# A graph layer on one core: transfers of the lengths moved to ScalarE, ten tiles fetched by rows, two hot quads summed last

## The chip, the core and the metric

The kernel runs on one core of a Trainium2 chip. A core has TensorE (PE, with its weight loads PEld), VectorE (DVE), ScalarE (ACT), GpSimd (POOL) and SyncE (SP). The metric is the device time of one execution in microseconds, less being better. Three runs of the kernel before took 719.8, 721.39 and 721.6 us, with a median of 721.39.

## The reference, cut to what matters

```python
width = CUTOFF / NUM_RBF * 0.5                    # 10 / 50 * 0.5
centers = jnp.linspace(0.0, CUTOFF, NUM_RBF)
rbf = jnp.exp(-(distances[:, None] - centers) ** 2 / (2.0 * width * width))
cut = 0.5 * (jnp.cos(jnp.pi * distances / CUTOFF) + 1.0) * (distances <= CUTOFF)
W = (silu(rbf @ fw1 + fb1) @ fw2 + fb2) * cut[:, None]
messages = (h[src] @ pw + pb) * W
agg = segment_sum(messages, dst, num_segments=num_atoms)
x = h + (silu(agg @ mw1 + mb1) @ mw2 + mb2)
out = (x - mean(x)) / sqrt(var(x) + 1e-05)        # over the last axis
```

There are 400,000 edges, sorted by `dst`, and 12,500 nodes of 128 numbers. An edge has a source, a destination and a length. Edges longer than 10 have `cut` 0 and add nothing. The weights are 128x128 (`fw1` is 50x128).

## The kernel before, in words

**Lists.** The edges come in seven chunks. For each chunk DVE finds the edges that are near enough and where each belongs in a shorter list; POOL scatters sources, destinations and lengths to a table `packed` in DRAM (L507); SP reads the shortened list back as `pair` (two transfers, L834); DVE unpacks it (`unpack`, which begins with `two`, L852, then L853), and SP stores the lengths as `near_d` in DRAM (L911). The table is cleared beforehand by transfers of zeros (`clear_packed`, L229). From here on edges stand in 139 quads, each four tiles of 128 edges. A chunk becomes 11 to 27 quads, and chunk 3 begins at quad 46, chunk 4 at 69, chunk 5 at 91, chunk 6 at 114.

**The loop over quads.** For a quad, POOL gathers the 128 projected source rows of each tile by an indirect transfer (`fetch`, L1074; the tables `proj`, or `in_x_dram` in the beginning). For the quads in `SINGLY` tile 0 is left out there; SP fetches its 128 rows instead, one transfer of 512 bytes each (`one_by_one`, L1064), and before each 32 of them loads 32 addresses into registers (L1060, TENSOR_LOAD). For each pair of quads (number `o`), SP fetches the lengths, spread over partitions (`radial`, L1093, the tile `d`, three buffers); ACT makes the radial basis (L1121, L1122); PE multiplies (L1130); ACT takes silu (L1136); PE makes the filter (L1144, L1147). DVE multiplies filter and gathered rows (`message`, L1158) and makes the one-hot matrix (`place`, L1170); PE sums (`sum_up`, L1190), and DVE adds the sum to the node's column (`add`, L1223). When a stretch of nodes has all its sums, the node stages follow (L1233 to L1292).

**What sets the order.** The order of instructions on each engine is written out (`manual_schedule`); an engine runs its list from first to last. A small planner in the code decides between which steps the rows of `one_by_one` stand: a clock in the planner adds `A_ROW` for each row. DVE's `two` of chunk 3 stands right after the message of quad 26, a full 20 quads before it is wanted. POOL's gathers each wait for a sum some steps back, and for the buffer they write.

**Completion semaphores.** Each transfer that SP or ACT issues signals one of eight semaphores, `DMAHW0` to `DMAHW7`. They are given out in turn, in the order in which the whole program is written, over both engines together; and a transfer is not issued before the last one that had the same semaphore has landed. So transfer number m waits for number m-8. In the rows below this wait stands in brackets.

Of the kernel before, what the change touches and what calls it, by code (L numbers as in the profile page):

```python
# [10 lines left out]
F32 = mybir.dt.float32  # L11
# [33 lines left out]
LAST = 26  # L45
# [11 lines left out]
OTHERS = 4, 5, 6, 7  # L57
OWN_4 = 66
# [13 lines left out]
SINGLY = (22, 44, 62, 67, 86, 102, 118, 133)  # L72
A_ROW = .58
# [6 lines left out]
READY = {80: 9, 84: 6, 88: 5, 90: 4}  # L80
# [6 lines left out]
def kernel(  # L87
# [61 lines left out]
    def load_x(t0, n=None):  # L149
        t = x4_sb[loaded[0] % X_BUFS]  # L150
        loaded[0] += 1
        node_dma(t0, t, x, False, n)
        x_sb[t0] = t
# [26 lines left out]
    def quad_of(q):  # L180

        return q if q < LAST or q >= NL else LAST if q == NL - 1 else q + 1

    def steps(k):

        return k if k <= LAST or k >= NL else k - 1

# [35 lines left out]
    def clear_packed(k, eng):  # L223
        a, b = CLEAR[k:k + 2]
        for i in range(LISTS if k == 0 else 3):
            v = packed[i, a:b].rearrange("(p w) -> p w", p=P)
            for w0 in range(0, (b - a) // P, 376):
                n = min(376, (b - a) // P - w0)
                eng.dma_start(v[:, w0:w0 + n], zero_i[:, :n])  # L229
# [594 lines left out]
    def unpack(c):  # L824
# [109 lines left out]
        if mine:  # L934
            at_row = work.tile([64, P], I32, name="at_row", bufs=2)
            nc.vector.tensor_scalar(at_row[:np_], f_src[:, :P], float(4 * H), None, op0=OP.mult)
            for q in mine:
                p = 2 * (quad_of(q) - QB[c])
                singles.extend((q, e, at_row[p:p + 1]) for e in range(P))
# [17 lines left out]
        if QB[c] <= LAST < QB[c + 1]:  # L957
            k = 2 * (LAST - QB[c])
            upto, that = (work.tile([64, 1], F32, name=n, bufs=1)[:np_] for n in ("upto", "that"))
            nc.vector.scalar_tensor_tensor(that, ident[:np_, k:k + 1], -1.0, ident[:np_, k + 1:k + 2],  # L960
                                           op0=OP.mult, op1=OP.subtract)
# [87 lines left out]
    singles, alone, rows_at, row_at = [], {}, [], [0.0]  # L1049
# [38 lines left out]
    def radial(o, lengths, eng=nc.sync):  # L1088

        n = math.prod(lengths.shape) // QE  # L1090
        d = work.tile([P, QE], F32, name="d", bufs=3)
        v = lengths.rearrange("(o h) e -> o h e", o=1)
        eng.dma_start(d, v.to_broadcast([64, 2, QE]))  # L1093
        d_of[o] = d, n
# [3 lines left out]
    def radials(to):  # L1098

        while next_o[0] < min(to, -(-NL // 2)):  # L1100
# [3 lines left out]
            a, b = 2 * quad_of(quads(o)[0]), 2 * quad_of(quads(o)[-1]) + 2  # L1104
            assert b - a == 2 * len(quads(o))
            radial(o, near_d[a:b].rearrange("(h t) e -> h (t e)", t=2))
# [99 lines left out]
    def bases_of(q0, q1):  # L1206

        _, v = nc.values_load_multi_w_load_instructions(
            base_i[0:1, 2 * quad_of(q0):2 * quad_of(q1 - 1) + 2], engines=[mybir.EngineType.DVE],
            min_val=0, max_val=N - min(wide(q) for q in range(q0, q1)),  # L1210
            skip_runtime_bounds_check_because="bases are destinations, and end in the table")
        for k in range(2 * (q1 - q0)):
            bases[q0 + k // 2, k % 2] = v[k]

    def added(q):

        return max((q - 2) // 2 * 2 if q < NL - 14 else q - 1 if q < NL - 4 else q, 0)
# [85 lines left out]
    def finish(every):  # L1303

        for t0 in every:
            load_x(t0)
# [5 lines left out]
            normalize(*ready.pop(0), on=range(QT))  # L1312
# [33 lines left out]
    def nodes(q):  # L1346
# [21 lines left out]
        if q == NL - 7:  # L1368
            st_of[3] = statistics()
            node_stats(80, st_of[3])  # L1370
        if q == NL - 4:
            node_stats(84, st_of[3][:, 4:])
        if q == NL - 3:
            node_stats(88, st_of[3][:, 8:])
# [3 lines left out]
    def last_step(q, msg):  # L1378

        assert not ready and not deep and not singles  # L1380
        bases_of(q, NL - 1)
        roots = deviations([84, 88, 90], st_of[3][:, 4:])
# [3 lines left out]
        keep_busy(5)  # L1386
        sum_up(q, msg)
        assert done_to(2 * q + 2) >= 95 * P
        node_first(93)
# [7 lines left out]
        node_first(95)  # L1397
        last(1)
        normalize(*ready.pop(0))
# [339 lines left out]
```

## Time and profile before

| | |
|---|---|
| runs | 719.8, 721.39, 721.6 us |
| the profiled execution | 719.15 us, span 717.5 us |
| granted TensorE clock | 0.917 |
| PE, PEld | 590.3 us (82%), 465.0 us (65%) |
| DVE | 561.8 us (78%) |
| ACT | 397.3 us (55%) |
| POOL | 536.4 us (75%) |
| gathers of POOL (L1074) | 548 |
| rows fetched by SP (L1064) | 1024 |
| transfers of `d` (L1093) | 70, all on SP |

The span is counted from the first to the last instruction; the time of the execution is 1.65 us longer. Busy time of an engine leaves out the issuing of transfers on SP and ACT, register work and waits. "SPq" and "ACTq" are the queues on which these engines issue transfers. A wait is put down to the work that ended last before it.

### The profile page before, as it was taken

To read this page: it belongs to the slowest core of one execution; us is meant where nothing else is said; L and a number is where in the kernel's file an instruction comes from. 1 tells how busy PE (TensorE), PEld (TensorE's weight loads), DVE (VectorE), ACT (ScalarE), POOL (GpSimd) and SP (SyncE) were. 2 spreads that over 40 slices of the span, in tenths; PEclk is the share of its full clock that TensorE was granted. 3 is DMA by queue.
4 is the path that set the end of the run, shared out by engine and by line. 5 is a ranking of instruction groups with operands and counts; after the bars stand their busy time and mean duration, and the time that the engine had idled before them with its cause. 6 is when DMAs were issued, how large, how long until landed. Compare 5 with 4: busy or idle time off the path is not lost. (4 is left out here: it accounts for less than half of the span.)

```text
span 717.5 us, 13667 instructions
## 1 busy us (share of the span) xinstructions
PE 590.3 (82%) x3524; PEld 465.0 (65%) x3524; DVE 561.8 (78%) x1736; ACT 397.3 (55%) x564; POOL 536.4 (75%) x576
## 2 busy tenths in 40 slices
PE   6887877898889889888588896999987878878884
PEld 5775556776667667576466674787765655656663
DVE  8899799787988999899689895878655455565685
ACT  6557624563645566464348253858744833574474
POOL 7777777777777777777777777777777777777773
PEclk9999687997988999999979997999998999999998
DMA  8995442343334334343333343444433433244342
GB/s 263 348 324 174 149 128 75 87 137 100 98 86 121 97 95 108 97 128 83 94 106 113 98 119 103 137 127 135 136 97 99 148 92 114 84 141 134 96 130 91
DMA packets 53389, 91.35 MB, mean 127 GB/s; under 512 B 13856, under 2 KB 21120, under 8 KB 53306
## 3 DMA queue, kind: packets, MB, share of 16 engines
q1 hardware_dynamic: 34754, 53.20, 22.9%
q0 software_dynamic: 17840, 36.77, 19.8%
q8 instruction: 29, 0.48, 0.3%
q10 hardware_dynamic: 712, 0.46, 0.2%
q14 instruction: 54, 0.44, 0.2%
HBM read 74.59 MB, written 15.79 MB: 126 GB/s over the span
## 5 line engine op out<-in xcount | busy, mean ns | idle before, releaser
L1074 POOL DMA_INDIRECT quad<-proj,srci x421 | 400.6, 952 | 128.4 <-issue 97.6
L1147 PEld LDWEIGHTS bank<-fw_sb,s 128*128 128x128 f32 x1112 | 160.8, 208 | 66.5 <-issue 59.8
L1136 ACT ACTIVATE s<-ph 128x1024 f32<-128x1024 f32 x70 | 71.3, 1018 | 184.4 <-PE ph L1130 184.3
L1147 PE MATMUL bank<-fw_sb,s 128*128 128x128 f32 x1112 | 161.8, 293 | 0.0
L1130 PE MATMUL ph<-rbf,w_sb 102*128 102x512 f32 x278 | 147.1, 655 | 7.5 <-ACT rbf L1122 3.9
L1190 PEld LDWEIGHTS sums<-hot,msg 128*128 128x128 f32 x816 | 112.0, 204 | 54.9 <-issue 27.4
L1170 DVE TENSOR_SCALAR hot<-iota_n,dl,cut 128x80 f32<-128x80 f32 (+4 forms) x408 | 110.1, 344 | 23.6 <-PE sums L1190 21.7
L1190 PE MATMUL sums<-hot,msg 128*128 128x80 f32 (+4 forms) x816 | 113.7, 285 | 15.4 <-DVE msg L1156 7.7
L1144 PE MATMUL bank<-fb_b,ones_b 96*128 96x512 bf16 x139 | 56.1, 404 | 48.8 <-DVE msg L1158 29.8
L1074 POOL DMA_INDIRECT x<-proj,srci x79 | 75.0, 949 | 24.1 <-issue 19.8
L1158 DVE TENSOR_TENSOR msg<-bank,quad 128x512 f32<-128x512 f32 (+1 forms) x82 | 55.7, 679 | 39.4 <-DMA quad<-proj,srci 36.9
L1130 PEld LDWEIGHTS ph<-rbf,w_sb 102*128 102x128 f32 x278 | 52.8, 211 | 48.1 <-issue 38.8
L1223 DVE TENSOR_TENSOR aggT<-aggT,sums 128x80 f32 (+4 forms) x209 | 54.0, 258 | 32.5 <-PE bank L1234 11.7
L1121 ACT ACTIVATE rbf<-d,rbf_bias,rbf_scale 102x512 f32<-102x512 f32 x70 | 56.2, 803 | 14.8 <-DMA d<-near_d 14.7
L1074 POOL DMA_INDIRECT quad<-in_x_dram,srci x48 | 47.6, 992 | 14.8 <-issue 11.9
L347 PEld LDWEIGHTS bank<-pw_sb,xT 128*128 128x128 f32 (+1 forms) x292 | 42.0, 207 | 8.0 <-issue 4.0
L1122 ACT ACT_TABLE_LOAD x35 | 44.9, 1283 | 0.6
L1136 ACT ACT_TABLE_LOAD x35 | 44.9, 1283 | 0.6
L1122 ACT ACTIVATE rbf<-rbf 102x512 f32<-102x512 f32 x70 | 44.1, 630 | 1.5
L1190 PE MATMUL sums<-quad,quad 128*128 128x104 f32 (+3 forms) x296 | 40.9, 281 | 3.9 <-DVE quad L1158 3.9
L1170 DVE TENSOR_SCALAR quad<-iota_n,dl,cut 128x104 f32<-128x104 f32 (+3 forms) x148 | 40.5, 348 | 3.9 <-issue 2.8
L1158 DVE TENSOR_TENSOR quad<-bank,quad 128x512 f32<-128x512 f32 (+2 forms) x40 | 25.2, 632 | 23.4 <-DMA quad<-proj,srci 16.1
(282 smaller groups left out, 803.0 us busy)
## 6 DMA issues: line engine op xcount, KB each, us to landing
d<-near_d SPq DMA_DIRECT2D x70, 256.0 KB
dl<-proj SPq DMA_DIRECT2D x1024, 0.5 KB
x<-in_x_dram SPq DMA_DIRECT2D x45, 256.0 KB
quad<-proj,srci POOLq DMA_INDIRECT x421
proj<-hp SPq DMA_DIRECT2D x24, 256.0 KB
out_dram<-x SPq DMA_DIRECT2D x21, 256.0 KB
r_d<-in_edge_weight_dram SPq DMA_DIRECT2D x5, 256.0 KB
r_dst<-in_dst_dram SPq DMA_DIRECT2D x5, 256.0 KB
```

What stands on the lines that cost most here:

```text
L347: nc.tensor.matmul(to[:m, k, :], lT[:, k * P:k * P + m], w, start=False, stop=(k == a + c - 1))
L1074: ins = nc.gpsimd.indirect_dma_start(out=got[:, j, :], out_offset=None, in_=proj if table is None else table, in_offset=bass.IndirectOffse ...
L1121: nc.scalar.activation(rbf[:u], d[:u], AF.Square, bias=rbf_bias[:u], scale=rbf_scale[:u])
L1122: nc.scalar.activation(rbf[:u], rbf[:u], AF.Exp, scale=-1.0 / (2.0 * width * width))
L1130: nc.tensor.matmul(ph[:, h, :], w1_sb[:2 * KR, h, :], rbf[:2 * KR], start=True, stop=True)
L1136: nc.scalar.activation(s[:, :n], ph[:, :n], AF.Silu)
L1144: nc.tensor.matmul(pu, ones_b[:, :P], bias_b["fb2"].rearrange("k j f -> k (j f)"), start=True, stop=False)
L1147: nc.tensor.matmul(pu[:, j * H:(j + 1) * H], s[:, j * P:(j + 1) * P], fw2_sb, start=False, stop=(j == QT - 1))
L1158: nc.vector.tensor_mul(msg[:, a:b, :], pu_of[q].rearrange("p (j f) -> p j f", j=QT)[:, a:b, :], got_of[q][:, a:b, :])
L1170: nc.vector.tensor_scalar(hot[:, j, :wide(q)], iota_n[:, :wide(q)], dl[:, at[0], at[1]], cut[:, at[0], at[1]], op0=OP.is_equal, op1=OP.mult)
L1190: ins = nc.tensor.matmul(pa[:, k * W:k * W + wide(q)], msg[:, j, :], hot[:, j, :wide(q)], start=(j % n == 0), stop=(j % n == n - 1))
L1223: nc.vector.tensor_add(to, to, pa[:, k * W:k * W + wide(q)])
```

## The change

The text has five parts.

1. `SINGLY` grows from eight quads to ten, at other places; `A_ROW` goes from .58 to .48. SP then fetches the rows of ten tiles, 1280 in all, instead of 1024, and POOL makes two gathers fewer, 546 instead of 548.
2. `radial` issues the transfer of `d` from ACT for o >= 8, and one step earlier (`q // 2 + 6`).
3. `clear_packed` clears the same columns of all its lists with one transfer from zeros that are read over and over: 14 transfers become 4.
4. Two quads (25 and 26) are summed last instead of one (26). Both add to one window of the node columns, in node tile 3 (`END`).
5. The tail after the last quad is rewritten: the node tiles 93 and 95 are done before the last sum, the last tile's bias and doubled input are put into PSUM beforehand, and its normalization uses one statistic, one root, one reciprocal and one TENSOR_SCALAR.

The diff, cut:

```diff
-LAST = 26
+LAST = 25
+N_LAST = 2
+OWN_D = 8
-SINGLY = (22, 44, 62, 67, 86, 102, 118, 133)
-A_ROW = .58
+SINGLY = (22, 34, 43, 60, 74, 86, 99, 113, 126, 137)
+A_ROW = .48
-READY = {80: 9, 84: 6, 88: 5, 90: 4}
+READY = {80: 9, 84: 7, 88: 6, 90: 5, 93: 4, 95: 3}
...
     def clear_packed(k, eng):
         a, b = CLEAR[k:k + 2]
-        for i in range(LISTS if k == 0 else 3):
-            v = packed[i, a:b].rearrange("(p w) -> p w", p=P)
-            for w0 in range(0, (b - a) // P, 376):
-                n = min(376, (b - a) // P - w0)
-                eng.dma_start(v[:, w0:w0 + n], zero_i[:, :n])
+        m = LISTS if k == 0 else 3
+        v = packed[:m, a:b].rearrange("s (p w) -> p s w", p=P)
+        for w0 in range(0, (b - a) // P, 376):
+            n = min(376, (b - a) // P - w0)
+            eng.dma_start(v[:, :, w0:w0 + n], zero_i[:, None, :n].to_broadcast([P, m, n]))
...
     def radial(o, lengths, eng=nc.sync):
-        n = math.prod(lengths.shape) // QE
         d = work.tile([P, QE], F32, name="d", bufs=3)
-        v = lengths.rearrange("(o h) e -> o h e", o=1)
-        eng.dma_start(d, v.to_broadcast([64, 2, QE]))
-        d_of[o] = d, n
+        for h, v in enumerate(lengths):
+            v = v.rearrange("(o h) e -> o h e", o=1)
+            if len(lengths) == 1:
+                eng.dma_start(d, v.to_broadcast([64, 2, QE]))
+            else:
+                eng.dma_start(d[h::2], v[:, 0, :].to_broadcast([64, QE]))
+        d_of[o] = d, sum(math.prod(v.shape) for v in lengths) // QE
...
-            radial(o, near_d[a:b].rearrange("(h t) e -> h (t e)", t=2))
+            at = [quad_of(q) for q in quads(o)]
+            by = at[-1] - at[0] if len(at) > 1 else 1
+            v = near_d.rearrange("(h t) e -> h (t e)", t=2)
+            radial(o, [v[at[0]:at[-1] + 1:by]] if by > 0 else [v[a:a + 1] for a in at],
+                   nc.scalar if o >= OWN_D else nc.sync)
...
-        radials(q // 2 + 5)
+        radials(q // 2 + 6)
...
-    def last_step(q, msg):
+    def last_step(q):
-        bases_of(q, NL - 1)
-        roots = deviations([84, 88, 90], st_of[3][:, 4:])
+        node_second(95)
+        node_stats(95, st_of[1][:, 11:])
+        msg = message(q)
+        nc.scalar.activation(warm, half_pi, AF.Sqrt)
+        roots = deviations([84, 88, 90, 93, 95], st_of[1])
...
-        node_stats(93, st_of[1], lambda: add(NL - 1))
-        node_first(END)
-        node_stats(95, st_of[1][:, 2:])
-        node_second(END)
-        node_stats(END, st_of[1][:, 5:])
-        scales(*deviations([93, 95, END], st_of[1]))
-        normalize(*ready.pop(0), on=(0, 1), v=nc.gpsimd)
-        normalize(*ready.pop(0), on=(0, 1), eng=nc.scalar)
-        normalize(*ready.pop(0), on=(0,))
+        add(NL - 1)
+        nc.tensor.matmul(pz[:, :P], mw1_sb, aggT[:, END * P:(END + 1) * P], start=False, stop=True)
+        zs = work.tile([P, QE], F32, name="zs", tag="hp", bufs=3)[:, :P]
+        nc.scalar.activation(zs, pz[:, :P], AF.Silu)
+        nc.tensor.matmul(py[:, :H], zs, mw2_sb, start=False, stop=True)
+        st, mv = keep.tile([P, 6], F32, name="st_end"), keep.tile([P, 2], F32, name="mv_end")
+        nc.vector.bn_stats(st, py[:, :H])
+        nc.vector.bn_aggr(mv, st)
+        dev = keep.tile([P, 2], F32, name="dev_end")
+        nc.scalar.activation(dev[:, 0:1], mv[:, 1:2], AF.Sqrt, bias=eps)
+        nc.vector.reciprocal(dev[:, 1:2], dev[:, 0:1])
+        nc.vector.tensor_scalar(end_sb[:, 0, :], py[:, :H], mv[:, 0:1], dev[:, 1:2],
+                                op0=OP.subtract, op1=OP.mult)
```

Where instructions come to stand is seen at three places. The first is ACT at the silus of the pairs o = 14 and 15, half-way through chunk 2. Before (`s` is the result of silu, `ph` its input, `rbf` the basis):

```order
L1136 ACTIVATE s<-ph 128x1024 [waits PE_49] x2
L1121 ACTIVATE rbf<-d,rbf_bias,rbf_scale 102x512 [waits DMAHW3_49]
L1122 ACT_TABLE_LOAD
L1122 ACTIVATE rbf<-rbf 102x512 [waits Activation_49]
L1121 ACTIVATE rbf<-d,rbf_bias,rbf_scale 102x512 [waits DMAHW4_49]
```

After, with the transfers of `d` for o = 17, 18 and 19 among them (numbers 305, 317 and 409 in the count of all transfers):

```order
L1103 DMA d<-near_d 128x1x512 [waits DMAHW1_49]
L1150 ACT_TABLE_LOAD
L1150 ACTIVATE s<-ph 128x1024 [waits PE_49] x2
L1103 DMA d<-near_d 128x1x512 [waits DMAHW5_49]
L1135 ACTIVATE rbf<-d,rbf_bias,rbf_scale 102x512 [waits DMAHW7_49]
L1136 ACT_TABLE_LOAD
L1136 ACTIVATE rbf<-rbf 102x512 [waits Activation_49]
L1135 ACTIVATE rbf<-d,rbf_bias,rbf_scale 102x512 [waits DMAHW1_49]
L1136 ACTIVATE rbf<-rbf 102x512 [waits Activation_49]
L242 ACTIVATE aggT<-iota_n 128x500 [waits DVE_49]
L1103 DMA d<-near_d 128x1x512 [waits DMAHW1_49]
```

The transfer of pair 18 stands behind the silus of pairs 14 and 15, and that of pair 19 behind two bases more; each waits for a transfer of SP.

The second place is SP at the same part of the program. After, these are its rows numbered 309 to 317 (`dl` is the buffer of rows); the row left out waits for `DMAHW4` once more:

```order
L1073 DMA dl_171<-proj 1x512 [waits DMAHW4_49]
L1073 DMA dl_171<-proj 1x512 [waits DMAHW6_49]
L1073 DMA dl_171<-proj 1x512 [waits DMAHW7_49]
L1073 DMA dl_171<-proj 1x512 [waits DMAHW0_49]
L1073 DMA dl_171<-proj 1x512 [waits DMAHW1_49]
L1073 DMA dl_171<-proj 1x512 [waits DMAHW2_49]
L1073 DMA dl_171<-proj 1x512 [waits DMAHW3_49]
...
L1073 DMA dl_171<-proj 1x512 [waits DMAHW5_49]
```

Between the first and the second row `DMAHW5` is left out: it is the transfer of pair 18 on ACT. Eight rows behind the first SP comes to `DMAHW5` itself, and this row (transfer 325) waits for the landing of pair 18. From it to the transfers of `pair` for chunk 3 (394 and 395) stand 69 transfers, all of them rows, and two TENSOR_LOADs; then:

```order
L1073 DMA dl_171<-proj 1x512 [waits DMAHW1_49]
L837 DMA pair<-packed 32x3x512 [waits DMAHW2_49,DMASW1_49]
L837 DMA pair<-packed 14x3x512 [waits DMAHW3_49]
L1073 DMA dl_171<-proj 1x512 [waits DMAHW4_49]
L1073 DMA dl_171<-proj 1x512 [waits DMAHW5_49]
```

Before, the same place reads as follows, with the transfer of `d` on SP itself; 229 rows stand ahead of the `pair` of chunk 3 there, and 277 in the changed kernel:

```order
L1064 DMA dl_171<-proj 1x512 [waits DMAHW1_49]
L834 DMA pair<-packed 32x3x512 [waits DMAHW2_49,DMASW2_49]
L834 DMA pair<-packed 14x3x512 [waits DMAHW3_49]
L1093 DMA d<-near_d 128x1x512 [waits DMAHW4_49,Activation_49]
L1064 DMA dl_171<-proj 1x512 [waits DMAHW5_49]
```

Between the two kernels SP keeps its order of rows and `pair`, but the `d` leaves its list, and more rows stand ahead of the `pair`.

In the same way `pair` of chunk 4 (transfers 563 and 564), 5 (741 and 742) and 6 (932 and 933) stand behind rows that wait for the `d` of pairs 27 (516), 36 (688) and 45 (868); the `d` after those have the numbers 583, 759 and 952. At the end, the `d` of pair 69 is 1377, and the last row is 1509.

The third place is the end of DVE's list. Before (`dev` is the root, `end` the last node tile):

```order
L1223 TENSOR_TENSOR aggT<-aggT,sums 128x80
L1259 BN_STATS st<-x_89 128x6 x2
L1254 SCALAR_TENSOR_TENSOR x_90<-x_90,bank_169 128x256
L1254 SCALAR_TENSOR_TENSOR x_90<-x_90,bank_169 84x128
L1259 BN_STATS st<-x_90 128x6 x2
L1259 BN_STATS st<-x_90 84x6
L1254 SCALAR_TENSOR_TENSOR end<-end,bank_170 128x128
L1259 BN_STATS st<-end 128x6
L1266 TENSOR_TENSOR dif<-st 128x6
L1267 TENSOR_TENSOR both_m<-st 128x12
L1268 SCALAR_TENSOR_TENSOR dif<-dif 128x6
```

After:

```order
L1172 TENSOR_TENSOR quad_79<-bank_168,quad_86 128x128
L1228 ISA
L1228 TENSOR_TENSOR aggT<-aggT,sums 128x80
L1427 BN_STATS st_end<-bank_170 128x6
L1428 BN_AGGR mv_end<-st_end 128x2
L1431 RECIPROCAL dev_end<-dev_end 128x1
L1432 TENSOR_SCALAR end<-bank_170,mv_end,dev_end 128x128
```

Between the last addition and the last tile's output there are four instructions of DVE where there were some seventeen, with the other tiles' work moved ahead of the last message.

More of the change, by code (lines that the diff above doesn't have):

```diff
@@ L1204, in base_of @@
             bases[q, k] = v[0]
[L1206 to L1213, printed above, removed]
     def added(q):
[L1217 removed]
+        return max((q - 2) // 2 * 2 if q < NL - 14 else q - 1 if q < NL - 5 else q, 0)
     def add(q, ks=(0, 1)):
```

85 lines of the change are left out of this document (51 added, 34 removed).

## The prediction

> **What bounds the kernel now.** I read the page first, then the waits, then the stages, then the order of time where the change cuts in. The page gives shares of the span, and its costliest group.
>
> ```profile
> PE 590.3 (82%) x3524; PEld 465.0 (65%) x3524; DVE 561.8 (78%) x1736; ACT 397.3 (55%) x564; POOL 536.4 (75%) x576
> L1074 POOL DMA_INDIRECT quad<-proj,srci x421 | 400.6, 952 | 128.4 <-issue 97.6
> ```
>
> No engine is at its limit by busy time. The waits (engine, line, what was waited for: us, times, longest) say more:
>
> ```profile
> POOL quad L1074 <- issue: 109.5, 359, 0.3
> DVE msg L1158 <- DMA quad<-proj,srci: 36.9, 17, 4.0
> ACT rbf L1121 <- DMA d<-near_d: 14.7, 7, 6.4
> DVE two L852 <- DMA pair<-packed: 9.3, 3, 5.5
> ```
>
> POOL's gaps are 0.3 us each and never longer: it waits for nobody, and gathers without a break. The windows show it from first gather to last, and then what DVE does in four stretches (start:end, length, busy of the engines):
>
> ```profile
> 4.80:704.60 699.80, 523.22 (x548) 0.92 0.44 128
> 150.00:300.00 150.00, 128.90 (x751) 103.11 (x750) 135.19 (x386) 83.51 (x102) 113.51 (x120) 0.89 0.37 104
> 300.00:450.00 150.00, 121.62 (x705) 94.54 (x704) 126.97 (x373) 74.00 (x91) 113.58 (x120) 0.90 0.37 105
> 450.00:600.00 150.00, 132.24 (x803) 101.34 (x802) 95.57 (x338) 94.60 (x136) 113.72 (x120) 0.97 0.42 123
> 600.00:704.60 104.60, 85.37 (x500) 64.24 (x498) 65.70 (x227) 56.26 (x88) 79.25 (x84) 0.95 0.40 115
> ```
>
> A gather costs 523.22/548 = 0.95 plus 0.30, or 1.25 us, and 548 of them are the span up to 704.6. In the first two stretches DVE is 90% and 85% busy (135.19 and 126.97 of 150) and gathered tiles wait for it; later it drops to 64%, and DVE waits for gathers. So POOL sets the end as long as DVE never falls so far behind that all buffers are full. POOL's reserve against that I estimate from the order of time at 3 to 5 us around 220 and 440 to 500 us, and 8 to 12 elsewhere.
>
> **SP, which the change loads.** The rows that follow are SP's queue in order of time (start, length, engine, line, count), first a stretch with nothing between, then one with a TENSOR_LOAD in it, then the surroundings of a `d` and of chunk 3's `pair`.
>
> ```profile
> 99.89 4.42 SPq L1064 DMA_DIRECT2D dl<-proj  x14
> 92.89 7.23 SPq L1064 DMA_DIRECT2D dl<-proj  x15
> 187.64 0.52 SPq L1093 DMA_DIRECT2D d<-near_d  x1
> 188.26 5.48 SPq L1064 DMA_DIRECT2D dl<-proj  x15
> 193.84 0.52 SPq L1093 DMA_DIRECT2D d<-near_d  x1
> 203.53 0.79 SPq L834 DMA_DIRECT2D pair<-packed  x2
> L1060 SPq TENSOR_LOAD <-at_row x32: 2084/2174/2613, 74.8 to 644.8; - x32
> SPq L1064 <- DMA d<-near_d: 14.2, 29, 2.0
> ```
>
> One row is (4.42 - 0.23)/13 = 0.322 us. A TENSOR_LOAD is 2.17. The last line is the ring of eight semaphores at work: 29 times a row stood still until a `d` issued eight places earlier had landed. From the 15 rows at 188.26, which take 5.48 instead of 0.23 + 14 x 0.322 = 4.74, one `d` lands about 0.62 + 7 x 0.322 + 0.74 = 3.6 us after its issue. Today that costs little, because SP issues `d` itself and goes on at once.
>
> **The move of `d` to ACT.** It takes 62 transfers x 0.52 = 32 us off SP's issue time and puts them on ACT, which is 55% busy and mostly waits for PE; this I cost at nothing. But a `d` on ACT stands behind silus that wait for PE, which waits for DVE's pace, and the numbers of the ring run over both queues. SP may not pass a `d` of ACT by more than seven transfers until it has landed. Between `d` 18 (transfer 317) and chunk 3's `pair` (394) stand 69 rows that may only start once `d` 18 has landed. Here is when ACT got to the silu behind which each critical `d` is put, when DVE came to `two`, and the `pair` before the last one of these:
>
> ```profile
> 210.35 1.02 ACT L1136 ACTIVATE s<-ph 128x1024 f32<-128x1024 f32 x1 [2.66 <-PE ph L1130]
> 212.18 0.41 DVE L852 TENSOR_TENSOR two<-pair 46x256 int32<-46x256 int32 x1
> 272.71 1.02 ACT L1136 ACTIVATE s<-ph 128x1024 f32<-128x1024 f32 x1 [2.15 <-PE ph L1130]
> 282.55 0.46 DVE L852 TENSOR_TENSOR two<-pair 44x256 int32<-44x256 int32 x1 [0.24 <-DMA dl<-proj]
> 348.91 1.02 ACT L1136 ACTIVATE s<-ph 128x1024 f32<-128x1024 f32 x1 [2.97 <-PE ph L1130]
> 356.84 0.42 DVE L852 TENSOR_TENSOR two<-pair 46x256 int32<-46x256 int32 x1 [5.50 <-DMA pair<-packed]
> 430.05 0.71 SPq L834 DMA_DIRECT2D pair<-packed  x2
> 431.76 0.63 ACT L1122 ACTIVATE rbf<-rbf 102x512 f32<-102x512 f32 x1
> 434.75 0.46 DVE L852 TENSOR_TENSOR two<-pair 54x256 int32<-54x256 int32 x1 [3.31 <-DMA pair<-packed]
> ```
>
> From `pair` to `two` it is 434.75 - 430.05 = 4.7 us when DVE waits. Then:
>
> Chunk 3: `d` 18 issued at 211.4 and landed at 215.0; 69 rows x 0.322 + 2 x 2.17 = 26.6; `pair` at 241.6, `two` at 246.3 instead of 212.2, 34 us late. Chunk 4: `d` 26 after the silu of 272.71, at 274; 15 rows and a load until `d` 27 may go, at about 285; landed 288.6; 39 rows and a load, 14.7; `two` at 308 instead of 282, 26 late. Chunk 5: `d` 36 at 349.9, landed 353.5; 45 rows and a load, 16.7; `two` at 375 instead of 357, 18 late. Chunk 6: `d` 45 behind a basis that ends at 432.4, landed 436; 56 rows and a load, 20.2; `two` at 461 instead of 435, 26 late.
>
> DVE runs in order: behind `two` stand the messages and additions of all quads, and PE, ACT and POOL follow them through buffers. `near_d`, which feeds the `d` of the coming quads, is late by as much, but inside the same stop. The stops add to 34 + 26 + 18 + 26 = 104 us, each counted from the shifted time of the one before. Two things come off. POOL's reserve is spent once, 4 us. And after each stop PE and ACT have done work ahead, so DVE can run at its busy time alone: in 150 to 450 it was idle for 38 of 300 us, of which I let half, 19, come back (nothing to 38 are the ends). So the gathers shift by 104 - 4 - 19 = 81 us, with 62 to 100 as the range if the stops are as worked out.
>
> **Ten tiles by rows.** Two gathers fewer are 2 x 1.25 = 2.5 us saved at POOL's pace. 256 more rows are 256 x 0.322 + 8 x 2.17 = 100 us on SP, against 32 freed. In the last third the same ring holds the rows of quads 99, 113, 126 and 137. The clearest is the last: `d` 69 stands behind a basis on ACT, and 125 transfers with four loads follow it.
>
> ```profile
> L1064 SPq DMA_DIRECT2D dl<-proj x1024: 227/228/617, 77.5 to 660.7; - x171
> 657.29 1.28 ACT L1136 ACT_TABLE_LOAD   x1
> 701.67 0.69 DVE L1158 TENSOR_TENSOR msg<-bank,quad 128x512 f32<-128x512 f32 x1
> ```
>
> That basis ended where the table load of the last-but-one row begins, at 657.3, so the last row is issued at 657.8 + 3.6 + 125 x 0.322 + 4 x 2.17 = 710.3 and lands about 2.5 us later, while the message of quad 137 stood at 701.67: 11 us late. The other three I bound by nothing (buffers cover it) and 20 us (the 18, 20 and 15 us that the same count gives, less a reserve of 8 to 12 each); I take 9. Together 20.
>
> **Clearing and the two hot quads.**
>
> ```profile
> 82.11 2.85 SPq L229 DMA_DIRECT2D packed<-zero_i  x6
> ```
>
> The 10 transfers fewer free 10 x 2.85/6 = 5 us of SP near 80 us, where nothing waits for it; nothing. The hot quads move places and keep their work; nothing, with POOL's gathers as cover, and at most the two additions of 0.3 us each.
>
> **The tail.**
>
> ```profile
> 703.62 0.94 POOL L1074 DMA_INDIRECT quad<-proj,srci  x1 [0.30 <-issue]
> 705.60 0.77 DVE L1158 TENSOR_TENSOR quad<-bank,quad 128x128 f32<-128x128 f32 x3
> 708.08 0.30 PEld L1190 LDWEIGHTS sums<-quad,quad 128*128 128x128 f32 x2
> 708.58 0.24 DVE L1223 TENSOR_TENSOR aggT<-aggT,sums 128x80 f32 x1 [0.80 <-PE sums L1190]
> 709.75 1.28 ACT L1270 ACT_TABLE_LOAD   x1
> 713.96 0.40 SPq L178 DMA_DIRECT2D out_dram<-end  x1
> ```
>
> Now the last sum starts at 708.08, 1.7 us after the last message (705.60 + 0.77), behind node work of other tiles on PE, and the last store 0.8 behind others. With these gone, and with fewer small DVE operations, but with the table load (1.28) still in the chain, the store comes about 3 us earlier. Ends: 0 and 5.
>
> **Sum**, against the profiled execution's 719.15 us: + 81 + 20 - 2.5 - 3 = 815. The median of the runs, 721.39, lies 2.2 above that execution, so I say **817**.
>
> **Rivals.** *POOL stays the bound (faster).* If ACT issues each `d` early enough, all that is left is 721.4 - 2.5 - 3 = 716. For it speaks that ACT is 55% busy and that the transfers are asked for one step earlier; it holds if `d` 18 is issued by 212.2 - 4.7 - 26.6 - 3.6 = 177 us. Against it: ACT's list has it behind the silu that ran at 210.35.
> The Trainium skill speaks for this rival: "DMA: Bandwidth & Descriptors", "Issuing engines are not separate DMA queues", says that issuing from several engines saves only the sequencer's time for it. By that the move would be worth 32 us of SP, off the path, and the time 716; no run here shows it with `d` on ACT. [...]
>
> *Only SP's rows are late.* Without the ring, SP has 1280 x 0.322 + 40 x 2.17 = 499 us of rows for 700 - 77 = 623. In the kernel before, 1024 rows took from 77.5 to 660.7, 0.57 each; at that pace 1280 end at 807, at the pace of 0.39 that it can keep long before 700. Halfway, 0.49, they end at about 704, 3 us beyond the last message, and the time is about 719 to 735.
>
> *Stops half hidden.* If work ahead and shorter stops (rows faster than 0.322, DVE work that the planner puts before `two`) give back half, gathers shift by 40: 721 + 40 + 0 to 10 - 5.5 = 755 to 765. For it: DVE also has node and pack work that might stand ahead; against: the list has `two` right behind a message.
>
> *It doesn't do what it says.* The `d` might land later from ACT, and SP, which only needed 14.2 us of waits for them, gain nothing: no gain, as in the second rival.
>
> **Chances.** Stops as worked out, 770 to 855: 0.62. Half hidden, 735 to 770: 0.17. Rows late alone, 719 to 735: 0.07, of which 0.03 within 0.3% of before, about what this measurement can tell from no change (2.2 us). POOL the bound, 713 to 718: 0.12. Beyond 855: 0.02. The range leaves out the faster case and the second rival, and reaches from the bottom of the half hidden case to 817 + 19 (nothing given back) + 14 for three late tiles and the tail: 738 to 850. Faster 0.13, same 0.03, slower 0.84.
>
> **What the profile will show.** Right: waits of `two` on `pair` for 15 to 35 us at three or four places; SP's rows waiting for `d` in long single waits; ACT's `d` issues waiting for `dl`; gaps of POOL before gathers, for sums or messages; DVE's busy share under 70%. A tail of about 10 us from last gather to last store. Wrong, if `two` waits no more than 6 us: then ACT issued in time, and POOL's row again shows gaps of 0.3 alone. If the stops are there and POOL has no gaps, my estimate of its reserve is the wrong step.

## The result

The changed kernel takes **910.32 us** (median of 6 runs, 906.17 to 915.38) where the kernel before took 721.13 beside it: a ratio of 1.2624, with a 95% interval from 1.2581 to 1.2666. The prediction said slower, by the mechanism that the trace then shows, but 817 us with 850 as its upper end. Of a loss of 189 us it had found 96. Runs more than 1.5% above the fastest of their kernel are left out of the times and ratios below.

Busy time hardly moved. From the page of the profile after, and then POOL's line from the page before:

```profile
span 911.0 us, 14117 instructions
PE 604.8 (66%) x3529; PEld 476.8 (52%) x3529; DVE 560.8 (62%) x1737; ACT 397.4 (44%) x566; POOL 531.7 (58%) x571
POOL 7777775777137741776067532777477577646020
```

```profile
POOL 7777777777777777777777777777777777777773
```

Every engine does the work it did, within 15 us, in a span that is 193 us longer. The POOL lines are its busy share, in tenths, in 40 equal slices of the span (22.8 us after, 17.9 before): where the kernel before has one 7 after another, there are holes now, and they lie at the stops that are listed below. The waits after:

```profile
POOL quad L1083 <- issue: 169.9, 385, 26.0
DVE two L855 <- DMA pair<-packed: 60.0, 3, 29.1
DVE two L855 <- DMA dl<-proj: 53.7, 2, 32.4
DVE x L1259 <- DMA x<-in_x_dram: 45.7, 4, 28.1
SPq L1073 <- DMA d<-near_d: 203.7, 52, 11.4
```

SP's rows stood still 203.7 us for transfers of `d`, against 14.2 before. DVE's `two` waited 113.7 us in five waits for the list of its chunk (three are put down to `pair`, two to a row that landed beside it), against 9.3. And one wait is new: the node stages (L1259) waited 45.7 us for the nodes' own input `x`, which SP loads too.

DVE in order of time, its waits of over 7 us for a transfer from quad 26 on; the last bracket is the idle time ahead:

```profile
253.84 0.42 DVE L855 TENSOR_TENSOR two<-pair 46x256 int32<-46x256 int32 x1 [32.43 <-DMA dl<-proj]
325.20 0.29 DVE L1170 TENSOR_TENSOR msg<-bank,dl 128x128 f32<-128x128 f32 x1 [7.32 <-DMA dl<-proj]
350.16 0.42 DVE L855 TENSOR_TENSOR two<-pair 44x256 int32<-44x256 int32 x1 [21.27 <-DMA dl<-proj]
450.44 0.42 DVE L855 TENSOR_TENSOR two<-pair 46x256 int32<-46x256 int32 x1 [23.14 <-DMA pair<-packed]
555.08 0.42 DVE L855 TENSOR_TENSOR two<-pair 54x256 int32<-54x256 int32 x1 [29.05 <-DMA pair<-packed]
652.79 0.29 DVE L1170 TENSOR_TENSOR quad<-bank,dl 128x128 f32<-128x128 f32 x1 [20.11 <-DMA dl<-proj]
727.47 0.29 DVE L1170 TENSOR_TENSOR msg<-bank,dl 128x128 f32<-128x128 f32 x1 [21.80 <-DMA dl<-proj]
781.33 0.69 DVE L1259 SCALAR_TENSOR_TENSOR x<-x,bank 128x512 f32<-128x512 f32 x1 [11.25 <-DMA x<-in_x_dram]
806.10 0.29 DVE L1170 TENSOR_TENSOR quad<-bank,dl 128x128 f32<-128x128 f32 x1 [11.82 <-DMA dl<-proj]
860.53 0.69 DVE L1259 SCALAR_TENSOR_TENSOR x<-x,bank 128x512 f32<-128x512 f32 x1 [28.07 <-DMA x<-in_x_dram]
```

The first stop can be followed from end to end, on ACT, SP and POOL:

```profile
206.34 0.52 ACTq L1103 DMA_DIRECT2D d<-near_d  x1
219.51 1.02 ACT L1150 ACTIVATE s<-ph 128x1024 f32<-128x1024 f32 x1 [2.66 <-PE ph L1144]
219.51 0.52 ACTq L1103 DMA_DIRECT2D d<-near_d  x1
258.18 0.62 ACT L242 ACTIVATE aggT<-iota_n 128x500 f32<-128x500 f32 x1 [33.65 <-DVE aggT L1228]
258.19 0.52 ACTq L1103 DMA_DIRECT2D d<-near_d  x1
196.45 53.90 SPq L1073 DMA_DIRECT2D dl<-proj  x113
250.45 0.79 SPq L837 DMA_DIRECT2D pair<-packed  x2
260.98 0.94 POOL L1083 DMA_INDIRECT quad<-proj,srci  x1 [27.75 <-PE sums L1204]
```

The `d` of pair 17 is issued at 206.3, that of pair 18 at 219.5, with the silu that PE released. Up to 250 SP issues rows and nothing else. Its waits from 196 to 251 us:

```profile
SPq L1073 <- DMA d<-near_d: 14.1, 3, 8.9
```

The longest, 8.9 us, ends when a `d` lands. Behind the rows comes `pair`, and `two` at 253.84, 32.4 us late (the prediction had 34). POOL, whose next gather has to wait for a sum of PE, stops for 27.8.

Here is where the loop stands in each kernel that is spoken of below: the start of the message of some quads (for a quad by rows, of its three gathered tiles), read from the order of time of DVE, in us.

| quad | before | after | e1: d on SP | e3: no rows | e9: tail alone | e10: d on ACT from pair 38 | e11: first six | e12: last four | e14: pair on ACT |
|---|---|---|---|---|---|---|---|---|---|
| 5 | 123.7 | 130.7 | 129.0 | 124.0 | 125.1 | 132.7 | 130.7 | 124.2 | 131.1 |
| 26 | 210.7 | 219.8 | 217.6 | 209.6 | 212.5 | 218.0 | 219.2 | 210.2 | 218.8 |
| 46 | 289.0 | 357.8 | 310.5 | 289.7 | 290.7 | 311.6 | 356.9 | 291.2 | 328.1 |
| 91 | 480.4 | 599.7 | 509.4 | 483.3 | 479.3 | 531.3 | 596.1 | 497.9 | 567.3 |
| 113 | 584.0 | 727.7 | 608.9 | 590.2 | 584.2 | 658.3 | 698.2 | 595.2 | 702.4 |
| 137 | 701.7 | 899.6 | 749.9 | 720.7 | 712.6 | 827.4 | 829.1 | 766.3 | 870.6 |

After against before: 7 us late at quad 5, 9 at 26, 119 at 91, 198 at 137; and what follows this message takes 11.4 us where it took 15.8.

### The profile page after: what moved, and what is told of

Its sections match the earlier page's. It is cut to its first block, busy times and chain, and to the rows that moved or that the text cites. A ratio compares the mean times of both kernels' runs of the same rounds, so it can differ in the third digit from the quotient of the medians.

```text
span 911.0 us, 14117 instructions
## 1 busy us (share of the span) xinstructions
PE 604.8 (66%) x3529; PEld 476.8 (52%) x3529; DVE 560.8 (62%) x1737; ACT 397.4 (44%) x566; POOL 531.7 (58%) x571
## 5 line engine op out<-in xcount | busy, mean ns | idle before, releaser
L1161 PEld LDWEIGHTS bank<-fw_sb,s 128*128 128x128 f32 x1112 | 165.9, 214 | 85.2 <-issue 79.1
L1161 PE MATMUL bank<-fw_sb,s 128*128 128x128 f32 x1112 | 166.0, 298 | 0.0
L1144 PE MATMUL ph<-rbf,w_sb 102*128 102x512 f32 x278 | 150.8, 669 | 8.9 <-ACT rbf L1136 5.0
L1184 DVE TENSOR_SCALAR hot<-iota_n,dl,cut 128x80 f32<-128x80 f32 (+4 forms) x408 | 109.1, 341 | 29.6 <-PE sums L1204 27.8
L855 DVE TENSOR_TENSOR two<-pair 44x256 int32<-44x256 int32 (+3 forms) x6 | 2.5, 416 | 113.8 <-DMA pair<-packed 60.0
L1204 PE MATMUL sums<-quad,quad 128*128 128x80 f32 (+3 forms) x296 | 41.4, 283 | 28.7 <-DVE quad L1170 26.3
L1204 PEld LDWEIGHTS sums<-quad,quad 128*128 128x128 f32 x296 | 38.3, 200 | 30.3 <-DVE quad L1170 26.7
L1243 ACT ACTIVATE zs<-bank 128x512 f32<-128x512 f32 (+3 forms) x27 | 14.7, 550 | 88.9 <-PE bank L1239 88.8
L1259 DVE SCALAR_TENSOR_TENSOR x<-x,bank 128x512 f32<-128x512 f32 (+3 forms) x27 | 16.5, 616 | 57.3 <-DMA x<-in_x_dram 45.7
L920 PE MATMUL bank<-ident,f_src 44*128 44x44 f32 (+3 forms) x12 | 2.6, 319 | 70.6 <-DVE f_src L887 33.1
```

What stands on the lines that cost most here:

```text
L1144: nc.tensor.matmul(ph[:, h, :], w1_sb[:2 * KR, h, :], rbf[:2 * KR], start=True, stop=True)
L1161: nc.tensor.matmul(pu[:, j * H:(j + 1) * H], s[:, j * P:(j + 1) * P], fw2_sb, start=False, stop=(j == QT - 1))
L1184: nc.vector.tensor_scalar(hot[:, j, :wide(q)], iota_n[:, :wide(q)], dl[:, at[0], at[1]], cut[:, at[0], at[1]], op0=OP.is_equal, op1=OP.mult)
L1204: ins = nc.tensor.matmul(pa[:, k * W:k * W + wide(q)], msg[:, j, :], hot[:, j, :wide(q)], start=(j % n == 0), stop=(j % n == n - 1))
L1259: nc.vector.scalar_tensor_tensor(y[:m, a:a + c], y[:m, a:a + c], 2.0, py[:m, a:a + c], op0=OP.mult, op1=OP.add)
```

## The experiments

Times are medians beside the kernel before on the same chip in the same session, which took 720.4 to 721.4 us in all but e5 to e8 and e16. In the two sessions of those five it took 1003 and 1016 us, so they are read against that alone, and the runs e9, e11, e12, e15 and e17 repeat them. Both ran under the same chip number as e13 to e15, where the kernel before took 721.33, so what made them slow stays open.

"The ring" is short for the eight completion semaphores that are given out in turn.

### e1: d back on SP

```diff
-OWN_D = 8
+OWN_D = 999
```

> The changed kernel with all transfers of d issued by SP again (ten tiles by rows, the clearing and the new tail stay). Ring theory (SP's rows stand still because each eighth transfer before them is a d that ACT has not issued yet): no stop of DVE's two on pair over 8 us, time 713 to 735. Rows theory (SP cannot deliver ten tiles by rows, whoever issues d): DVE still waits 10 us and more for rows in the last third, time over 760.

**765.67 us**, ratio 1.0635 (1.0587 to 1.0683). The waits of `two`:

```profile
DVE two L855 <- DMA pair<-packed: 32.4, 5, 9.4
```

Neither theory alone. 145 of the 189 us hang on who issues `d`; the waits of `two` shrink from 113.7 to 32.4 in all, the longest to 9.4, a little over the 8 that the ring theory allowed. The time is the one that the rows theory named (over 760), but not for its reason: DVE waits for no row in this run. So 45 us stay with `d` on SP: the ten tiles by rows and the rest of the change, which my sum without the ring has as a gain of 5.5.

### e2: d on ACT, and nothing else

In the kernel before:

```diff
-            radial(o, near_d[a:b].rearrange("(h t) e -> h (t e)", t=2))
+            radial(o, near_d[a:b].rearrange("(h t) e -> h (t e)", t=2), nc.scalar if o >= 8 else nc.sync)
```

> The kernel before with only this changed: d of the pairs o >= 8 issued by ACT. Between the last d ahead of each pair and that pair stand 34, 36, 31 and 22 transfers of SP for chunks 3 to 6, where the changed kernel has 69, 39 (behind 15 more), 45 and 56. Ring theory: stops shorter than there, 10 to 20 us at each chunk by 0.39 us a transfer and some 5 besides, and late rows afterwards; time 765 to 820. Rows theory: eight tiles as before, so no change, 719 to 726. Third theory (issuing on ACT is slow in itself): ACT busy or waiting at its own d, time anywhere over 730 with stops on d, not on pair.

**817.68 us**, ratio 1.1364 (1.1330 to 1.1398). In the order of time of DVE and the waits of SP:

```profile
231.31 0.42 DVE L852 TENSOR_TENSOR two<-pair 46x256 int32<-46x256 int32 x1 [18.36 <-DMA pair<-packed]
318.26 0.42 DVE L852 TENSOR_TENSOR two<-pair 44x256 int32<-44x256 int32 x1 [17.57 <-DMA pair<-packed]
401.92 0.42 DVE L852 TENSOR_TENSOR two<-pair 46x256 int32<-46x256 int32 x1 [16.50 <-DMA dl<-proj]
493.26 0.42 DVE L852 TENSOR_TENSOR two<-pair 54x256 int32<-54x256 int32 x1 [16.50 <-DMA pair<-packed]
```

```profile
SPq L1064 <- DMA d<-near_d: 193.2, 53, 12.7
```

The one edit costs 97 us and takes SP's waits for `d` from 14.2 to 193.2. With 34, 36, 31 and 22 transfers in the way the stops are 18.4, 17.6, 16.5 and 16.5, against 32.4, 23.1 and 29.1 where there were 69, 45 and 56: from this kernel to the changed one a stop grows with the transfers in the way, by about 0.4 us each on top of some 5. Inside this kernel that does not show: 36 transfers stop it for less than 34 do, and 22 for as long as 31.

### e3: no rows

```diff
-SINGLY = (22, 34, 43, 60, 74, 86, 99, 113, 126, 137)
+SINGLY = ()
```

POOL gathers all 556 tiles; nothing is left out of the computation.

> The changed kernel without any tile by rows (POOL gathers all 556), d still on ACT. Ring theory: with no rows between, a d of ACT and the pair after it are a few transfers apart, no stops of two on pair over 8 us; 10 more gathers at 1.25 us; time 722 to 735. Third theory (ACT's issuing or landing of d is what costs): stops stay, time over 760.

**735.06 us**, ratio 1.0209 (1.0180 to 1.0239). SP's waits for a list to be written, 21.5 us before, are now:

```profile
SPq L837 <- DMA packed<-line,at_i: 201.4, 4, 70.1
```

SP waits 201 us in all for lists that are not written yet, so it is ahead. With `d` on ACT and no rows `two` waits 4.7 us at the longest, and messages are 3 us behind the kernel before at quad 91. The 14 us that this run takes more than the kernel before are no more than its eight additional gathers (8 x 1.25 = 10) and the new tail (7, e9). So the move of `d` shows no cost of its own; it costs when rows of SP stand between.

### e4: ten tiles by rows, and nothing else

In the kernel before, with `d` on SP:

```diff
-SINGLY = (22, 44, 62, 67, 86, 102, 118, 133)
-A_ROW = .58
+SINGLY = (22, 34, 43, 60, 74, 86, 99, 113, 126, 137)
+A_ROW = .48
```

> The kernel before with the ten tiles by rows and the pace of the changed kernel, d on SP. Ring theory: no stops; two gathers fewer, 717 to 730, with at most some us for rows that come late near the end. Rows theory: over 760.

**751.51 us**, ratio 1.0428 (1.0370 to 1.0485). Between the two theories: no long stop, but 31 us lost for two gathers saved (the 32 of the next expectation counts a fourth run, 758.57).

### e8 and e15: nine tiles by rows

```diff
-SINGLY = (22, 44, 62, 67, 86, 102, 118, 133)
-A_ROW = .58
+SINGLY = (22, 38, 52, 66, 80, 94, 108, 121, 134)
+A_ROW = .52
```

> The kernel before with nine tiles by rows instead of eight (22, 38, 52, 66, 80, 94, 108, 121, 134, pace .52), d on SP. If what ten tiles cost (32 us with d on SP) grows with every tile: 730 to 742. If SP has room for nine: one gather fewer, 717 to 722.

> The kernel before with nine tiles by rows instead of eight (22, 38, 52, 66, 80, 94, 108, 121, 134, pace .52), d on SP. If what ten tiles cost (32 us with d on SP) grows with every tile: 730 to 742. If SP has room for nine: one gather fewer, 717 to 722.

e15: **727.96 us**, ratio 1.0086 (1.0061 to 1.0111); e8: 1.0192 (1.0116 to 1.0268). Nine tiles cost 7 us and ten cost 31, while each tile saves one gather of 1.25. The quads and the planner's pace change with the number in these runs, so what the number alone costs was not separated. The time lies between my two cases (717 to 722, 730 to 742), nearer the second.

### e5 and e9: the tail, the hot quads and the clearing alone

The changed kernel with

```diff
-OWN_D = 8
+OWN_D = 999
-SINGLY = (22, 34, 43, 60, 74, 86, 99, 113, 126, 137)
-A_ROW = .48
+SINGLY = (22, 43, 61, 66, 86, 102, 118, 133)
+A_ROW = .58
```

> The changed kernel with d on SP and eight tiles by rows at the old pace (quads 22, 43, 61, 66, 86, 102, 118, 133, .58): what is left of the change is the hot quads, the clearing and the new tail. My prediction's tail term: the same as before less 3 us, 715 to 719. Rival, from the run without rows, where the last gather ended at 713.9 and the end came 19.5 us later instead of 13.0: the new tail puts the node work of tiles 84 to 95 ahead of the last message and costs 6 us net, 723 to 729.

> Again the changed kernel with d on SP and eight tiles by rows at the old pace: what is left of the change is the hot quads, the clearing and the new tail. My prediction's tail term: 715 to 719 beside 721. Rival, from the run without rows (last gather to end 19.5 us, before 13.0): 723 to 729.

e9: **728.56 us**, ratio 1.0097 (1.0069 to 1.0125), as the rival had it. (e5, in a session of 1003 us, says 0.9928, 0.9877 to 0.9979; but there one kernel's runs spread from 985 to 1010, so it is not read as a gain.) The clearing and the two hot quads are in this run too and were not run by themselves. The loop is within 2 us of the kernel before up to quad 126 and loses 11 by quad 137. On ACT and DVE of e9:

```profile
696.60 0.31 ACT L1632 ACTIVATE end<-end 128x128 f32<-128x128 f32 x1 [3.98 <-DMA end<-in_x_dram]
696.82 0.47 ACT L1243 ACTIVATE zs<-bank 128x384 f32<-128x384 f32 x1
702.13 0.55 DVE L1259 SCALAR_TENSOR_TENSOR x<-x,bank 128x384 f32<-128x384 f32 x1 [6.87 <-PE bank L350]
```

The changed tail doubles the input of the last node tile on ACT, right after the place where SP is to fetch it. ACT waits 4 us for that transfer, the silu of a node stage stands behind it, PE's second product behind that, and DVE in order behind PE: 6.9 us, for a tile whose own turn comes at the very end.

### e13: the last tile's input earlier

In the kernel of e9:

```diff
+        if q == NL - 12:
+            node_dma(END, end_sb, x, False)
         if q == NL - 5:
-            node_dma(END, end_sb, x, False)
             nc.scalar.activation(end_sb, end_sb, AF.Copy, scale=2.0)
```

> The run with the tail alone (d on SP, eight tiles), with the transfer of the last node tile's input seven quads earlier; the doubling of it on ACT stays where it is. There ACT waited 4.0 us for this transfer at the doubling, the silu of a node stage stood behind it, and DVE waited 6.9 us for that stage. If that wait is what the new tail costs: 7 to 10 us faster than that run, 717 to 722 beside 721. If the node work moved ahead of the last message costs in itself: 726 to 730.

**723.18 us**, ratio 1.0036 (1.0019 to 1.0053): 5.4 us back, less than the 7 to 10 expected. The same two places (ACT no longer waits), the next node work on DVE, and the last message:

```profile
691.86 0.30 ACT L1633 ACTIVATE end<-end 128x128 f32<-128x128 f32 x1
695.87 0.56 DVE L1259 SCALAR_TENSOR_TENSOR x<-x,bank 128x384 f32<-128x384 f32 x1 [1.31 <-PE bank L350]
705.31 0.61 DVE L1259 SCALAR_TENSOR_TENSOR x<-x,bank 128x256 f32<-128x256 f32 x2 [2.41 <-PE bank L350]
710.30 0.28 DVE L1172 TENSOR_TENSOR quad<-bank,quad 128x128 f32<-128x128 f32 x1
```

The last message is done in pieces of one tile; from its last piece (710.30) to the end of the span (717.9) it is 7.6 us, and before (706.1 to 717.5) it was 11.4. So in these two traces the new tail saves 3.8 us behind the last message, near the 3 that I had put in, and gives them back ahead of it: the last message comes 4.2 later, behind the node work of two tiles.

### e16 and e17: the message before that node work

```diff
-        node_second(95)
-        node_stats(95, st_of[1][:, 11:])
         msg = message(q)
+        node_second(95)
+        node_stats(95, st_of[1][:, 11:])
```

> The run before with the early load, and in the tail the message of quad 137 ahead of the second node stage of tile 95 instead of behind it. There this stage (DVE waits 2.4 us for PE, then works 1.1) stood ahead of the message at 706.4, where the kernel before has it at 701.7. If this order is what the tail still costs: 2 to 4 us faster, 719 to 721.5, level with the kernel before or just under it. If the first stage of 95 on PE, which stays ahead, sets the time: no change, 722 to 724.

> Again the run with the early load and the message of quad 137 ahead of the second node stage of tile 95. If the order on DVE is what the tail still costs: 719 to 721.5 beside 721. If the first stage of 95 on PE sets the time: 722 to 724.

e17: **721.60 us** beside 720.39, ratio 1.0016 (1.0002 to 1.0031); e16 is unclear (0.9954, 0.9868 to 1.0039). Beside the kernel before it is 1.2 us over, where e13 was 1.9 over. The two intervals overlap, so a gain from this order is not shown. This is the fastest version with the new tail, within 0.3% of the kernel before; none beat it.

### e7 and e12: only the last four tiles by rows

In the changed kernel, with `d` on ACT:

```diff
-SINGLY = (22, 34, 43, 60, 74, 86, 99, 113, 126, 137)
+SINGLY = (99, 113, 126, 137)
```

> The changed kernel with d on ACT, and only the last four tiles by rows (99, 113, 126, 137). Ring theory: a pair of chunks 3, 4 and 5 stands 1 to 2 transfers behind a d of ACT, so no stops there over 6 us; chunk 6 has 10 rows and its pair in the way, a stop under 10; then late rows and late loads of x as in the changed kernel, where the messages lost another 78 us between quad 91 and 137; six gathers more; 780 to 810. If my prediction's term for late tiles (20 us) were right: 745 to 755.

> Again the changed kernel with d on ACT, and only the last four tiles by rows (99 to 137). Ring theory: no stop over 6 us at chunks 3, 4 and 5 and one under 10 at chunk 6; then late rows and late loads of x; six gathers more; 780 to 810. If my prediction's term for late tiles (20 us) were right: 745 to 755.

e12: **781.93 us**, ratio 1.0830 (1.0795 to 1.0865); e7: 1.0443 (1.0359 to 1.0526) beside 1003 us. The waits of DVE in e12:

```profile
DVE x L1259 <- DMA x<-in_x_dram: 70.3, 8, 17.8
DVE two L855 <- DMA pair<-packed: 24.8, 4, 15.7
```

No stop over 5 us at chunks 3 to 5, 15.7 at chunk 6 (I had said under 10). After that DVE waits for no late row; its long waits are for `x`, which SP loads too and which stands between the rows in its queue.

### e6 and e11: only the first six

```diff
-SINGLY = (22, 34, 43, 60, 74, 86, 99, 113, 126, 137)
+SINGLY = (22, 34, 43, 60, 74, 86)
```

> The changed kernel with d on ACT, and only the first six tiles by rows (22 to 86). All transfers up to the pair of chunk 6 have the same numbers as in the changed kernel. Ring theory: the same four stops of 20 to 32 us, messages 119 us late at quad 91 as there, but nothing late after it; four gathers more; 830 to 850. If the stops depended on the later rows: less than 800.

> Again the changed kernel with d on ACT, and only the first six tiles by rows (22 to 86). All transfers up to the pair of chunk 6 have the changed kernel's numbers. Ring theory: the same four stops of 20 to 32 us, messages 110 to 120 us late at quad 91, nothing late after it, four gathers more; 830 to 850.

e11: **849.13 us**, ratio 1.1775 (1.1734 to 1.1816); e6: 1.1128 (1.1055 to 1.1202) beside 1003 us. The stops at chunks 3 to 6 are 32.3, 7.4 + 21.1, 23.7 and 28.4, the changed kernel's own, and messages are 116 us late at quad 91. After that nothing more is lost but the tail.

### e10: d on ACT only from pair 38 on

```diff
-OWN_D = 8
+OWN_D = 38
```

> The changed kernel with d on SP up to pair 37 and on ACT from pair 38 on. Ring theory: two of chunks 3, 4 and 5 waits under 10 us, as in the run with all d on SP; from there on the transfers have the changed kernel's numbers (d 868 ahead of the pair 932), so chunk 6 stops for 20 to 30 us, and rows and x come late afterwards; time 765 for the ten tiles and the tail, 20 for chunk 6, 50 for the late rows, 815 to 850. If the stops came from ACT's issuing in general or from the count of rows: 765 or 910.

**841.69 us**, ratio 1.1665 (1.1624 to 1.1707). The order of time of DVE:

```profile
229.05 0.42 DVE L855 TENSOR_TENSOR two<-pair 46x256 int32<-46x256 int32 x1 [9.47 <-DMA pair<-packed]
303.63 0.42 DVE L855 TENSOR_TENSOR two<-pair 44x256 int32<-44x256 int32 x1 [7.19 <-DMA dl<-proj]
487.33 0.42 DVE L855 TENSOR_TENSOR two<-pair 54x256 int32<-54x256 int32 x1 [29.04 <-DMA pair<-packed]
789.21 0.69 DVE L1259 SCALAR_TENSOR_TENSOR x<-x,bank 128x512 f32<-128x512 f32 x1 [27.43 <-DMA x<-in_x_dram]
```

The stops at chunks 3 to 5 are down to 9.5, 7.2 and 3.4 us, near those of e1, with their `d` back on SP, and the one at chunk 6 is there as in the changed kernel (29.04 and 29.05; e11, with the same numbers up to there, has 28.4). With the same transfers in the same places of the ring, the same wait follows, at 487.33 and at 555.08. This is the run that ties a stop to the numbers and not to the length of SP's list.

### e14: ACT issues the lists too

In the changed kernel:

```diff
-            (nc.scalar if c < 1 else nc.sync).dma_start(t[a:b, :l1 - l0],
+            (nc.scalar if c < 1 or c >= 3 else nc.sync).dma_start(t[a:b, :l1 - l0],
```

> The changed kernel, d on ACT and ten tiles by rows, with one more move: ACT also issues the transfers of pair for chunks 3 to 6, so they no longer stand behind SP's rows; in the count they come 12, 2, 64 and 2 places behind the last d ahead of them, instead of 77, 47, 53 and 64. If the stops come from rows that must be issued between a d of ACT and the pair: two of chunks 3, 4 and 6 waits under 10 us, chunk 5 up to 25, and 50 to 90 us come back, 820 to 860. If d on ACT slows the loop in another way: 890 to 920.

**885.65 us**, ratio 1.2294 (1.2254 to 1.2334), a miss: 25 us come back where 50 to 90 were expected. DVE's waits and one place in its order of time:

```profile
DVE x L1259 <- DMA x<-in_x_dram: 84.4, 11, 28.6
DVE first L720 <- DMA r_dst<-in_dst_dram: 30.3, 2, 21.3
DVE two L855 <- DMA pair<-packed: 10.1, 2, 7.9
```

```profile
399.76 0.15 DVE L720 CAST first<-r_dst 128x1 f32<-128x1 int32 x1 [21.32 <-DMA r_dst<-in_dst_dram]
```

`two` no longer waits, as expected (113.7 us became 10.1). But the loop stops nearly as long for the next thing that stands in SP's queue: the raw destinations of a later chunk, then `x` (84.4 against 45.7), then rows. The list was only the first of SP's transfers to be missed. SP's rows still wait 169.7 us for `d` here (203.7 in the changed kernel), so whatever stands in its queue comes late.

## Why the prediction was wrong, point by point

**The mechanism of the stops was right.** SP's rows wait for a `d` that ACT has not issued, and `two` waits behind them. The four stops were worked out as 34, 26, 18 and 26 us, in sum 104, and measured 32.4, 28.6 (7.3 for a late row and 21.3), 23.1 and 29.1, in sum 113. e2, e3 and e10 show that stops of this length come with `d` on ACT and rows in between, and only there. That transfers which share eight semaphores are the link is what the built program says and what fits all of these; a kernel with the same queues and separate semaphores was not tried. Of the signs, the waits of `two`, the long waits of SP's rows (up to 11.4 us) and DVE's share (62%) came as said. The 10 us from last gather to last store did not: it is 29.6 (878.0 to 907.6).

Of the hardware the Trainium skill ("DMA: Bandwidth & Descriptors", "Issuing engines are not separate DMA queues") says that issuing from several engines saves only the sequencer's time for it. e2 is this case, and the one move costs 97 us. No run here speaks against the rule as to the transfers themselves; it does not count what waits for them. The faster rival (716 us), which that rule spoke for, is refuted.

**The step that failed** is the sum of what lies around the stops: what comes back after a stop, the late transfers of the last third, and the price of the ten tiles with `d` on SP. The tail, a smaller term, had the wrong sign.

*Half of DVE's idle time, 19 us, comes back, and POOL's reserve takes 4.* Nothing came back. The messages are 9 us late at quad 26 and 119 at quad 91, which is 110 more, while DVE is busy as long as before (233.2 us between these two messages before, 233.4 after). The small waits of DVE that were to give way to the work done ahead are waits for PE, and they did not shrink. Between the two messages, before and after:

```profile
DVE hot L1170 <- PE sums L1190: 8.4, 6, 3.1
DVE aggT L1223 <- PE bank L1234: 8.3, 5, 2.7
```

```profile
DVE hot L1184 <- PE sums L1204: 12.4, 7, 4.1
DVE aggT L1228 <- PE bank L1239: 7.7, 5, 2.4
```

That is 16.7 us before and 20.1 after. Another 9.0 of the idle time before were waits of `two` itself, which the stops replace. So 113 for the stops, less 9, and some 6 for these and other waits make the 110. A slower PE is not the reason: in the 46 us after the first stop its granted clock is 0.90 and it is busy for 39.3 us, and in the 46 us behind the same `two` in the kernel before (212 to 258) 0.93 and 39.7. The whole span's clock, 0.824 instead of 0.917, has the stops in it.

*Ten tiles by rows are 20 us late in the last third.* Between quads 91 and 137 the loop lost 198 - 119 = 79 us. Rows came 20.1, 21.8 and 11.8 us late at quads 99, 113 and 126. I had counted 18, 20 and 15 and then taken only 9 for the three, since buffers might cover them. And I had left out altogether what else stands in SP's queue behind rows: `x`, 45.7 us of waits of the node stages. Instead of quad 137's rows (11 us expected) it was the `x` ahead of it that came 28.1 us late. Rows and `x` make 99 us. Here some did come back: DVE's waits for gathered tiles fell from 53.0 us to 12.1 in this stretch, but its waits for PE grew by 19 (19.2 to 38.1).

*With two gathers fewer ten tiles gain, and with `d` on SP they cost at most 14 us.* With `d` on SP, ten tiles cost 751.51 - 720.97 = 31 us (e4), nine 7 (e15), though no `d` of ACT stands in the way there. What fits is that SP's rows stand ahead of lists and `x`: in e1 `two` waits 32.4 us (9.3 before) and the node stages 9.0 for `x`. It is seen from the start: in the changed kernel the list of chunk 2, before any `d` of ACT stands in its way, came 7.8 us late:

```profile
127.52 0.42 DVE L855 TENSOR_TENSOR two<-pair 44x256 int32<-44x256 int32 x1 [7.83 <-DMA pair<-packed]
```

**The tail**: 3 us saved by the prediction, 7.2 lost in e9. The saving is there (3.8, e13); a transfer asked for just before it is used (5.4, e13) eats it, and so, by the place of the last message, does the node work moved ahead of it. I had read the end of DVE's list, where the operations were fewer, and not the rows ahead of it, to which they had gone.

**How it adds up.** Along the loop the changed kernel loses 9 us up to quad 26, where nothing was put in, 110 from there to quad 91, where 81 were forecast, and 79 to quad 137, where 20 were; then it gains 4. So the late rows and `x` of the last third are the largest miss. By runs: the first six tiles with `d` on ACT cost 849.13 - 721.39 = 128 us with the tail (e11), the last four 60.5 with the tail (e12), the tail 7.2 (e9). 128 + 60.5 - 7.2 = 181 of 189; the rest appears only when both are there. By issuer: 145 for `d` on ACT (e1 against after), 7 for the tail (e9), and 37 left for the ten tiles, which alone in the kernel before cost 31 (e4).

One sentence ahead of the prediction was loose: the numbers of the ring are not given in the order of the code. The list of chunk 3 is written before the `d` of pair 18 (the built program names them 2997 and 3008), and stands in the ring at 394 and 317. They follow the order in which the framework lays out the whole program, and it puts ACT ahead of SP there. On the chip ACT was not ahead.

## What to carry to other kernels

Before a transfer is moved to another queue, look up which transfers share its completion semaphores, and count what stands between it and the next thing that an in-order engine will wait for; a queue with slack of its own can lose it to the pace of another engine. When one transfer in a queue is late, price every other transfer in that queue too: e14 moved the one that was waited for, and the next in line took its place. And do not price more small transfers in a queue by their issue time alone: here SP's was filled for an estimated 70% of the time (eight tiles and 70 `d`: 1024 x 0.322 + 32 x 2.17 + 70 x 0.52 = 435 of some 620 us, by the rows in the prediction), and nine tiles cost 7 us, ten 31.

## What the runs showed that was not expected

- A stop came out almost the same in kernels whose earlier parts differed by 68 us: 29.05 us at chunk 6, and 29.04 in e10. That the two agree to 0.01 us is luck; e11 has 28.42.
- By quad 91 nothing of the stops was caught up, though DVE was busy only 85 to 90% of the time in that part of the kernel before. Most of the rest was waits for PE and for the list, and the waits for PE did not get shorter.
- In two sessions the kernel before took 1003 and 1016 us instead of 721. In e5, from the first of them, the profile puts some of the longest waits down to "remote", a label that names no engine of the core (ACT's silu waited 154.4 us for it; e9, the same kernel, has no such wait). A saving of a few us could not be told there.
